# Expert matrices on ScalarE's DMA queue, a joint normalisation of two batches, and one value group per pair of heads, in a Macaron block with experts

## The chip, the cores and the metric

The kernel runs on one core of a Trainium2 chip. A core has five engines that each work through their own instructions in order: TensorE (PE) multiplies matrices and transposes, VectorE (DVE) and ScalarE (ACT) work on rows, GpSimd (POOL) does elementwise work and issues the indirect DMAs, and SyncE (SP) issues the other DMAs. "PEld" in the profile is PE's weight load, which overlaps its products. The engines wait for one another by semaphores. The metric is the device time of one execution in microseconds (us); the median of several runs is given.

## The reference

The input x is 4 batches of 512 rows of 256 numbers, all in float32. LN is a layer norm without weights.

```
x = x + 0.5 * FFN(LN(x));  x = x + ATT(LN(x));  x = x + 0.5 * FFN(LN(x))

FFN(x):  logits = x @ gate                      # 8 experts
         w, e = top_2(logits); w = softmax(w)
         out[row] = sum over its 2 experts of w * ((silu(x @ w0[e]) * (x @ w1[e])) @ wo[e])
                                                # w0, w1: 256x512; wo: 512x256
ATT(x):  q = rms_norm(x @ wq_a) @ wq_b          # 16 heads of 64 + 64 (rope)
         k, v from rms_norm(x @ wkv_a) @ wkv_b  # the rope part of k is shared by all heads
         out = softmax(rope(q) @ rope(k)^T * scale) @ v;   return out @ wo
```

## The kernel before, in words

**FFN.** Each of the two FFNs is worked as 39 tiles of 128 rows, all rows of a tile for one expert. Routing chooses two experts per row, counts the rows of each expert, and lists for each tile its row indices, weights and expert. It runs ahead of the tiles or beside them: for the first FFN batches 0 and 1 come first (`route_first`, L659), nine tiles made of them are begun, and `route_second` (L744) routes batches 2 and 3 beside these tiles. The list of the other 30 tiles can only be read after that.

`ffn_tiles` (L910) is a generator, one tile per step. `gather` (L919) reads the tile's row in the weights into a register, starts the DMAs of w0 and w1 of the expert (512 KB each) and has POOL gather the 128 rows `xg`. It is called two tiles ahead; three buffers hold the weights, so a tile's weights can start when the hidden products of the tile three before are done. `turn` (L946) transposes `xg`; `hidden` (L956) does 32 products into two PSUM tiles `h`, the silu on ACT (L973) and the product on DVE (L975); `project` (L978) does 8 products `py`, scales them on DVE (L998), and POOL adds the rows to `acc_d` in DRAM by an indirect DMA (L1003). `load_x` (L108) reads a batch's x back from `acc_d` on SP, which must wait for those additions. Near the end of the second FFN four DMAs (L1015) copy `acc_d` to the output; the last tiles are then added to the output itself.

**Attention.** An item is one head of one batch, and two items are a pair, with eight steps `at` = 0 to 7 (loop at L1338 to L1384). A step issues in this order: the score group of a row block one and a quarter heads ahead (`put_scores`; two products `ps`, then the negated maximum on DVE, L1163, and the exponential on ACT, L1166), the four transposes of one key chunk of the item's four divided row blocks (`turn_probs`, L1173, copied out of PSUM by DVE or ACT), in some steps the value products (`put_weigh`, L1242) or a half of an output projection (`put_out`), and the division of the row block just scored (`put_divide`: a reciprocal on DVE, L1170, and a multiplication on POOL, L1171). In the value products (`weigh`, L1187) two heads lie side by side in PE's columns, two products a key chunk. The chunks 0 and 1 of a pair are issued as a group at step 7 of the pair, the chunks 2 and 3 at step 1 of the next pair. Every second pair carries an output projection.

**Side work.** `Beside` (L313) holds generators: routing for the second FFN, normalisation of the next batch (`normed`, L411), its keys and values (`prepare`, L1061). Each `step()` lets the first generator issue its next piece. A piece that says `PE_NEXT` wants PE next, and is then let on only at the places given as `pe_places`. In attention there are one or two `step()` calls in each step, ten in a pair: at even steps after the division, at odd ones ahead of it, with a second one after it at steps 1 and 7. `asked` is a second such list, for the queries.

**Normalisation.** `normed` does the row statistics of a batch's four row blocks, an inverse square root by three Newton rounds on DVE (`inv_sqrt`, L362, lines 372 to 374), the normalised rows on DVE (first half) and ACT (second half), their stores to DRAM, the transposes, and the copies out of PSUM. `route_second` calls it for batch 2 and then for batch 3. `list_tiles` (L799) then sums the counts (`pn_c`, L820), and looks rows and weights up by products (`px`, from L876) in a table that it reads back from DRAM.

Of the kernel before, what the change touches and what calls it, by code (L numbers as in the profile page):

```python
# [9 lines left out]
F32 = mybir.dt.float32  # L10
# [6 lines left out]
P = 128  # L17
# [15 lines left out]
def kernel(  # L33
# [48 lines left out]
    tp = ctx.enter_context(tc.tile_pool(name="turned", bufs=1))  # L82
    tm = ctx.enter_context(tc.tile_pool(name="tmp", bufs=2))
    xp = ctx.enter_context(tc.tile_pool(name="xn", bufs=2))
# [3 lines left out]
    ptp = ctx.enter_context(tc.tile_pool(name="pt", bufs=2 * NT))  # L88
# [222 lines left out]
    PE_NEXT = "pe"  # L311

    class Beside:  # L313
        def __init__(self, pe_places=None):
            self.todo = []
            self.pe_places = pe_places
            self.count = self.until = self.place = 0
            self.pe = False

            self.quiet = True  # L320
# [9 lines left out]
        def step(self, n=1):  # L330

            for _ in range(n):
                if not self.todo or self.count < self.until:
                    return
                if self.pe and self.pe_places and self.place not in self.pe_places:
                    return
                said = next(self.todo[0], self)
                self.pe = said is PE_NEXT
                if said is self:
                    self.todo.pop(0)  # L340
                elif said is not None:
                    self.until = self.count + (1 if self.pe else said)
# [14 lines left out]
    def stats(mv, xt, t):  # L357
        sb = small.tile([P, 6], F32, tag="st", name="st")
        nc.vector.bn_stats(sb, xt[:, t, :])
        nc.vector.bn_aggr(mv[:, t, :], sb)  # L360
# [17 lines left out]
    def minus_mean(mv, rstd):  # L378
        less = small.tile([P, NT], F32, tag="less", name="less")
        nc.vector.scalar_tensor_tensor(less, mv[:, :, 0], -1.0, rstd, ALU.mult, ALU.mult)  # L380
        return less
# [29 lines left out]
    def normed(b, s, store=None, then=None, joint=False):  # L411
# [3 lines left out]
        for t in range(NT):  # L415
            stats(mv, xs[b], t)
            yield
# [128 lines left out]
    def choose(ph, s, lTs, b, cut):  # L546
# [47 lines left out]
        yield PE_NEXT  # L594
# [149 lines left out]
    def route_second(ph, listing):  # L744

        s = {}
        lTs = []
        for b in range(2, B):
            yield from normed(b, s, ph.f, joint=True)
            pl = ps_p.tile([P, P], F32, tag="p", name="pl")  # L750
            gate(pl, lambda t: s["xnT"][:, :, t * P : (t + 1) * P])
            lTs.append(ap.tile([P, P], F32, tag="o", name="lT"))
            nc.scalar.copy(lTs[-1], pl)
            yield
        nt = NT * len(lTs)
# [4 lines left out]
        for t in range(0, n, 2):  # L760
            for k in range(2):
# [10 lines left out]
                yield PE_NEXT  # L772
# [26 lines left out]
    def list_tiles(ph, n, m, split=0, read=None):  # L799
# [15 lines left out]
        def parts():  # L815
# [55 lines left out]
            yield PE_NEXT  # L871
# [38 lines left out]
    def ffn_tiles(f, jobs, final=None):  # L910
# [8 lines left out]
        def gather(j):  # L919
            if j >= n:  # L920
# [4 lines left out]
                engines=(mybir.EngineType.SP,),  # L925
# [5 lines left out]
            for w, src in enumerate((w0_k, w1_k)):  # L931
                nc.sync.dma_start(
                    w01[j][:, w],
                    src.rearrange("e k m -> (e k) m")[bass.ds(row, D), :].rearrange(
                        "(c p) m -> p c m", p=P
                    ),
                )
# [361 lines left out]
    beside.step(5)  # L1299
    next(tiles)  # L1300

# [3 lines left out]
    for j in tiles:  # L1305
# [11 lines left out]
        elif j > done + 3:  # L1317
            beside.step()
# [17 lines left out]
    beside.pe_places = None  # L1336
    late = []
    for i, (b, h) in enumerate(items):  # L1338
# [13 lines left out]
        for kc in range(NT):  # L1352
# [9 lines left out]
            if at == 1 and i > 0:  # L1362
                put_weigh(i - 1, (2, 3))
            elif at == 7:
                put_weigh(i, (0, 1))
# [7 lines left out]
            if kc % 2:  # L1373
                beside.step()
            else:
                asked.step()
            put_divide(k)
            if kc % 2:
                asked.step()
                if at in (1, 7):  # L1380
                    beside.step()
            else:
                beside.step()
# [3 lines left out]
    put_weigh(n_items - 1, (2, 3))  # L1387
# [6 lines left out]
    beside.pe_places = PE_PLACES  # L1394
# [76 lines left out]
```

## Time and profile before

| | |
|---|---|
| median of 3 runs | 1213.08 us (1212.36 to 1217.93) |
| the profiled execution | 1213.32 us, of which the span is 1211.3 |
| mean granted clock of PE | 0.969 |
| start to about 46 us | routing of batches 0 and 1, folding of weights |
| 46 to 305 us | first FFN's tiles |
| 317 to 943 us | attention: PE busy 595 of 626 us |
| 947 to 1199 us | second FFN's tiles: PE busy 231 of 252 us |
| hidden products `h`, L963 | 2496 matmuls, 300.9 us |
| scores `ps`, L1155 | 512 matmuls, 271.9 us |
| transposes `pt`, L1177 | 1024, 156.6 us |
| value products `po`, L1190 | 512, 126.1 us |
| weights of the tiles | 156 DMAs of 512 KB on SP's queue |

One line of a timeline is the start in us, the time taken, the engine, the line of the kernel, the operation, what it writes <- what it reads, the shape and the number of instructions put together; in brackets stands how long the engine had been idle before, and what ended that. "SPq" is SP issuing a DMA; the time is that of the issue, not of the transfer. The page's row "PEclk" shows the clock that PE was granted, in tenths of full speed, in 40 equal slices of the span.

### The profile page before, as it was taken

The numbers are of one execution on the slowest core, as the hardware profiler recorded it, in microseconds if no ns is written. First come the engines' busy times: TensorE is split into PE (matmuls) and PEld (weight loads), VectorE is DVE, ScalarE is ACT, GpSimd is POOL, SyncE is SP. The second block draws the span as 40 slices with busy tenths as digits, with TensorE's granted clock in tenths as the row PEclk, the third lists the DMA queues.
The fourth block names the chain that finished last, engine by engine and source line by source line (L and its number), as shares of the span: only waits on it lengthen the run. The fifth ranks groups of instructions, "written<-read, shape, count | busy, mean of one in ns | idle before, by whom it ended". The sixth has DMA issues, their size and how long they took to land. (4 is left out here: it accounts for less than half of the span.)

```text
span 1211.3 us, 18471 instructions
## 1 busy us (share of the span) xinstructions
PE 1107.8 (91%) x6264; PEld 775.0 (64%) x6264; DVE 612.3 (51%) x1677; ACT 406.0 (34%) x914; POOL 577.5 (48%) x645
## 2 busy tenths in 40 slices
PE   4888999799999999999899989999999997999795
PEld 3677999788545455444445545454445787999784
DVE  6463222234567556686657666666755332222121
ACT  4420111011454555453455544455544210101000
POOL 4244444345545554443565435573663254444242
PEclk8989999899999999998999989999999998999898
DMA  9776888665100000100000100000002587887762
GB/s 304 233 220 166 228 246 234 206 201 150 18 1 1 1 1 5 48 1 1 1 1 18 35 1 1 1 18 18 1 5 70 161 231 161 221 238 216 264 207 38
DMA packets 80365, 126.43 MB, mean 104 GB/s; under 512 B 13105, under 2 KB 36785, under 8 KB 80177
## 3 DMA queue, kind: packets, MB, share of 16 engines
q1 hardware_dynamic: 62816, 101.86, 25.7%
q0 software_dynamic: 17184, 23.39, 11.2%
q8 instruction: 51, 0.84, 0.3%
q14 instruction: 42, 0.34, 0.1%
q10 hardware_dynamic: 272, 0.01, 0.0%
HBM read 107.88 MB, written 21.54 MB: 107 GB/s over the span
## 5 line engine op out<-in xcount | busy, mean ns | idle before, releaser
L1171 POOL TENSOR_SCALAR pr<-pr,sm 128x512 f32<-128x512 f32 x256 | 177.8, 696 | 285.5 <-DVE sm L1170 246.4
L963 PE MATMUL h<-xT,w 128*128 128x128 f32 x2496 | 300.9, 280 | 14.1 <-DVE xT L954 5.7
L963 PEld LDWEIGHTS h<-xT,w 128*128 128x128 f32 x2496 | 297.7, 197 | 21.6 <-DVE xT L954 8.0
L1166 ACT ACTIVATE pr<-ps,nm 128x512 f32<-128x512 f32 x256 | 175.9, 687 | 304.5 <-DVE nm L1163 278.5
L1155 PE MATMUL ps<-k,q 128*128 128x512 f32 x512 | 271.9, 614 | 4.5 <-ACT pr L1166 4.5
L1177 PEld LDWEIGHTS pt<-ident,pr 128*128 128x128 f32 x1024 | 126.7, 141 | 157.0 <-issue 98.1
L1163 DVE TENSOR_REDUCE nm<-ps 128x1 f32<-128x512 f32 x256 | 174.7, 683 | 103.5 <-PE ps L1155 103.2
L1003 POOL DMA_INDIRECT acc_d<-yo,idx x64 | 102.0, 1593 | 200.7 <-DVE yo L998 140.8
L973 ACT ACTIVATE g<-h 128x512 f32<-128x512 f32 x78 | 46.5, 596 | 390.6 <-PE h L963 240.4
L975 DVE TENSOR_TENSOR it<-g,h 128x512 f32<-128x512 f32 x78 | 53.6, 687 | 242.8 <-PE h L963 205.0
L1177 PE MATMUL pt<-ident,pr 128*128 128x128 f32 x1024 | 156.6, 276 | 17.0 <-ACT pT L1184 13.8
L989 PE MATMUL py<-wo_sb,it 128*128 x624 | 152.7, 389 | 0.8 <-PE pt_x L951 0.2
L1155 PEld LDWEIGHTS ps<-k,q 128*128 128x128 f32 x512 | 79.7, 191 | 77.4 <-ACT pr L1166 39.4
L989 PEld LDWEIGHTS py<-wo_sb,it 128*128 128x128 f32 x624 | 115.1, 194 | 17.9 <-issue 4.4
L1190 PE MATMUL po<-pT,low 128*64 128x512 f32 x512 | 126.1, 615 | 0.0
L939 POOL DMA_INDIRECT xg<-xn_d,idx x78 | 77.7, 996 | 32.6 <-issue 20.6
L1170 DVE RECIPROCAL sm<-sm 128x1 f32<-128x1 f32 x256 | 41.2, 161 | 101.7 <-ACT pr L1166 101.3
L1182 DVE COPY pT<-pt 128x512 f32<-128x512 f32 x128 | 87.0, 680 | 2.2 <-PE pt L1177 2.2
L1184 ACT COPY pT<-pt 128x512 f32<-128x512 f32 x128 | 73.7, 575 | 2.9 <-PE pt L1177 2.9
L998 DVE TENSOR_SCALAR yo<-py,wt 128x256 f32<-128x256 f32 x78 | 37.7, 483 | 71.0 <-PE py L989 67.1
L1204 PE MATMUL pwo<-wvo,oT 128*128 128x256 f32 x256 | 65.4, 398 | 2.3 <-ACT oT L1252 2.3
L1190 PEld LDWEIGHTS po<-pT,low 128*64 128x64 f32 x512 | 31.6, 138 | 49.0 <-issue 49.0
(218 smaller groups left out, 1003.0 us busy)
## 6 DMA issues: line engine op xcount, KB each, us to landing
w<-in_L_ffn_w_kernel_dram SPq DMA_DIRECT2D x156, 512.0 KB
wo_sb<-in_L_ffn_wo_kernel_dram SPq DMA_DIRECT2D x4, 1024.0 KB
x<-_attn_hidden_states_dram SPq DMA_DIRECT2D x4, 512.0 KB
xn_d<-xn POOLq DMA_DIRECT2D x8, 256.0 KB
x<-acc_d SPq DMA_DIRECT2D x4, 512.0 KB
acc_d<-x SPq DMA_DIRECT2D x4, 512.0 KB
xn_d<-xn SPq DMA_DIRECT2D x8, 256.0 KB
out_dram<-acc_d SPq DMA_DIRECT2D x4, 512.0 KB
```

Of the source, the lines that this page charges most:

```text
L939: nc.gpsimd.indirect_dma_start(out=xg[j], out_offset=None, in_=xn_d[f][: res["rows"], :], in_offset=bass.IndirectOffsetOnAxis(ap=res["idx" ...
L963: nc.tensor.matmul(p[:, m, :], lhsT=w01[j][:, w, c, m * P : (m + 1) * P], rhs=xT[j][:, c, :], start=(c == 0), stop=(c == DC - 1),)
L989: nc.tensor.matmul(py, lhsT=it[:, m, :], rhs=wo_sb[:, bass.ds(off + m * D, D)], start=(m == 0), stop=(m == MC - 1),)
L1003: nc.gpsimd.indirect_dma_start(out=dst, out_offset=bass.IndirectOffsetOnAxis(ap=idx, axis=0), in_=y, in_offset=None, compute_op=ALU.add,)
L1155: nc.tensor.matmul(ps, lhsT=qT[:, t * P : (t + 1) * P], rhs=st[b]["k"][h % 2], start=True, stop=True,)
L1163: nc.vector.tensor_reduce(nm, ps, AX.X, ALU.max, negate=True)
L1166: nc.scalar.activation(pr, ps, AF.Exp, bias=nm, accum_out=sm)
L1171: nc.gpsimd.tensor_scalar(pr, pr, sm, 1.0, ALU.mult, ALU.mult)
L1177: nc.tensor.transpose(pt[:, t * P : (t + 1) * P], probs[t][:, kc * P : (kc + 1) * P], ident)
L1182: nc.vector.tensor_copy(s, pt)
L1184: nc.scalar.copy(s, pt)
L1190: nc.tensor.matmul(po[j * RANK : (j + 1) * RANK], lhsT=st[b]["low"][:, kc, 1, :], rhs=pts[j], start=(kc == 0), stop=(kc == NT - 1),)
```

## The change: what it does

- The register load and the two weight DMAs of a tile are issued by ACT instead of SP.
- `route_second` normalises batches 2 and 3 together: eight statistics, one inverse square root over eight columns, all eight normalised blocks, the four stores on SP; then the transposes of one batch after the other, all copied by ACT, and both gates. Two buffers more hold normalised rows, and one more the transposed ones.
- A second word for side work, `PE_LATE`, lets a piece on at the first of the `pe_places` alone. In `normed` the statistics are issued two at a time. Beside the first tiles eight pieces are let on before the first tile's step and three after it.
- All four key chunks of a pair's value products are one group, issued at step 0 of the next pair; one buffer more holds turned probabilities.
- Side work in attention is let on behind the division only, in the numbers `PARTS` for the eight steps (ten a pair, as before). Beside the last tiles of the first FFN and the tiles of the second, PE work of it is let on at one of a tile's places (1) instead of two (1 and 3).

```
-    tp = ctx.enter_context(tc.tile_pool(name="turned", bufs=1))
+    tp = ctx.enter_context(tc.tile_pool(name="turned", bufs=2))
-    xp = ctx.enter_context(tc.tile_pool(name="xn", bufs=2))
+    xp = ctx.enter_context(tc.tile_pool(name="xn", bufs=4))
-    ptp = ctx.enter_context(tc.tile_pool(name="pt", bufs=2 * NT))
+    ptp = ctx.enter_context(tc.tile_pool(name="pt", bufs=2 * NT + 1))
...
-                if self.pe and self.pe_places and self.place not in self.pe_places:
-                    return
+                if self.pe and self.pe_places:
+                    n_ok = 1 if self.pe is PE_LATE else len(self.pe_places)
+                    if self.place not in self.pe_places[:n_ok]:
+                        return
...
     def route_second(ph, listing):
         s = {}
+        bs = range(2, B)
+        n = NT * len(bs)
+        mv = small.tile([P, n, 2], F32, tag="mv2", name="mv2", bufs=1)
+        for i in range(n):
+            stats(mv, xs[2 + i // NT], i % NT, i)
+            yield
...
+        yield from inv_sqrt(rstd, var, n)
+        less = minus_mean(mv, rstd)
...
+                store_rows(nc.sync, ph.f, b, half, xn[b, half])
...
+        for b in bs:
+            yield PE_LATE if b == 2 else PE_NEXT
+            for half in range(2):
+                pt = ps_p.tile([P, DC, H2 * P], F32, tag="p", name="pt_ln")
+                turn_rows(pt, xn[b, half])
+                xnT[b, half] = pt
+            yield
...
+                nc.scalar.copy(t[:, :, half * H2 * P : (half + 1) * H2 * P], xnT[b, half])
...
+        yield PE_LATE
-        for b in range(2, B):
-            yield from normed(b, s, ph.f, joint=True)
+        for b in bs:
             pl = ps_p.tile([P, P], F32, tag="p", name="pl")
...
-                engines=(mybir.EngineType.SP,),
+                engines=(mybir.EngineType.Activation,),
...
-                nc.sync.dma_start(
+                nc.scalar.dma_start(
                     w01[j][:, w],
...
     beside.at(0)
-    beside.step(5)
+    beside.step(8)
     next(tiles)
+    beside.step(3)
...
         elif j > done + 3:
-            beside.step()
+            beside.pe_places = PE_PLACES[:1]
+            beside.step(2)
...
+    PARTS = (4, 2, 1, 1, 0, 0, 1, 1)
+    beside.pe_places = ()
...
-            if at == 1 and i > 0:
-                put_weigh(i - 1, (2, 3))
-            elif at == 7:
-                put_weigh(i, (0, 1))
+            if at == 0 and i > 0:
+                put_weigh(i - 1, range(NT))
...
-            if kc % 2:
-                beside.step()
-            else:
+            if kc % 2 == 0:
                 asked.step()
             put_divide(k)
             if kc % 2:
                 asked.step()
-                if at in (1, 7):
-                    beside.step()
-            else:
-                beside.step()
+            beside.step(PARTS[at])
...
-    beside.pe_places = PE_PLACES
+    beside.pe_places = PE_PLACES[:1]
```

## The prediction

> **What bounds the kernel now.** I read the page first, then the busy times by stretch, then the timelines of TensorE (PE), of SyncE (SP), and of all engines at the places where PE stood still.
>
> ```profile
> span 1211.3 us, 18471 instructions
> ...
> PE 1107.8 (91%) x6264; PEld 775.0 (64%) x6264; DVE 612.3 (51%) x1677; ACT 406.0 (34%) x914; POOL 577.5 (48%) x645
> ...
> PEclk8989999899999999998999989999999998999898
> ```
>
> PE is the bound, and what a change of order can win is PE's idle time (its gaps sum to 90.9 us) and half clock. The stretches say where:
>
> ```profile
> 50.00:100.00 50.00, 42.14 (x296) 38.56 (x295) 29.42 (x117) 9.64 (x16) 22.87 (x29) 0.90 0.76 214
> ...
> 150.00:200.00 50.00, 50.00 (x382) 48.12 (x381) 13.79 (x28) 5.38 (x9) 23.50 (x19) 1.00 0.89 239
> 200.00:250.00 50.00, 43.61 (x311) 40.64 (x310) 16.29 (x48) 5.74 (x10) 18.06 (x14) 0.93 0.74 211
> ...
> 544.46:573.70 29.24, 26.38 (x98) 14.24 (x96) 17.96 (x43) 12.03 (x29) 10.29 (x13) 0.88 0.00 1
> 615.20:631.26 16.06, 15.97 (x69) 7.42 (x68) 9.74 (x22) 9.15 (x23) 12.71 (x18) 1.00 0.02 2
> ```
>
> Columns: window, length, busy PE, PE weight load, DVE, ACT, POOL, granted clock, DMA share, GB/s. From 150 to 200 us the FFN tiles leave PE no gap and nothing can be won; the first tiles and the tiles at 200-250 do. In attention a pair of heads with no side work has no gap either (615.20), but one beside the next batch's normalisation takes 29.24 at a clock of 0.88.
>
> The stops in the FFN stages, from the timelines of PE and SP (bracket: idle time before and what ended it):
>
> ```profile
> 64.49 3.81 PE L963 MATMUL h<-xT,w 128*128 128x128 f32 x32 [2.47 <-DVE newton L373]
> ...
> 220.39 0.37 SPq L110 DMA_DIRECT2D x<-acc_d  x1
> 221.34 2.47 SPq L932 DMA_DIRECT2D w<-in_L_ffn_w_kernel_dram  x4
> ...
> 233.37 0.69 PE L951 MATMUL pt_x<-ident,xg 128*128 128x128 f32 x2 [6.07 <-DMA xg<-xn_d,idx]
> ...
> 1022.61 0.59 PE L820 MATMUL pn_c<-ones,wide 128*128 128x1 f32 x2 [2.71 <-DVE wide L817]
> ```
>
> The name at 64.49 misleads: the tile's second weights landed at 64.3. At 220 the weights of a tile stand on SP behind an x load that waited for a scatter; at 226.79 the next gather was issued with 2 MB of weights in flight.
>
> The end of a quiet pair, all engines:
>
> ```profile
> 628.07 0.68 DVE L1163 TENSOR_REDUCE nm<-ps 128x1 f32<-128x512 f32 x1
> ...
> 628.43 1.94 PE L1190 MATMUL po<-pT,low 128*64 128x512 f32 x8
> ...
> 628.84 0.69 ACT L1166 ACTIVATE pr<-ps,nm 128x512 f32<-128x512 f32 x1 [0.44 <-DVE nm L1163]
> ...
> 629.65 0.16 DVE L1170 RECIPROCAL sm<-sm 128x1 f32<-128x1 f32 x1 [0.31 <-ACT pr L1166]
> 629.99 0.69 POOL L1171 TENSOR_SCALAR pr<-pr,sm 128x512 f32<-128x512 f32 x1 [0.37 <-DVE sm L1170]
> ...
> 630.30 1.12 PE L1155 MATMUL ps<-k,q 128*128 128x512 f32 x2
> ...
> 631.26 0.60 PE L1177 MATMUL pt<-ident,pr 128*128 128x128 f32 x4
> ```
>
> The first transposes of the next pair need the fourth divided row block, ready at 629.99 + 0.69 = 630.68. PE reaches them at 631.26: slack 0.58. What filled the time was the value group at 628.43.
>
> **The change part by part**, against the profiled execution, 1213.3 (span 1211.3 and 2.0 around it; the median, 1213.08, is 0.2 less).
>
> *A. First tiles.* From 46 to 118 us PE loses 13.3 in gaps and some 7 to half clock. One chain of Newton steps for two batches puts the listing of the remaining tiles about one tile earlier. In the changed program's order the third pair of weight loads is now on ACT ahead of the first silu; it waits for the second wne and nwq loads, which landed at 59.6 and 60.9. So the first silu comes at about 61 instead of 48.49, and the second half of tile 1's hidden products waits for PSUM until about 63: nearly what tile 2 lost before (64.49). Then each further step runs beside a 5.5 us tile, and tile 7's hidden products, at 111.62 (half clock until 113.2), start at about 104. That is -9; taking 2 off because four extra stores and all eight transpose copies are new on SP and ACT: -7, between -11 and 0. ACT's issue itself is about 0.27 + 2 x 0.42 = 1.1 us a tile (its only DMA before took 0.416) on an engine busy for 5.4 of 50 us at 150-200: hidden; uncovered only where it waits.
>
> *B. Tiles at 211-233.* Weights no longer stand behind the x loads: they go out when slots come free, at about 216.2 and 221.7, and the gather finds less in flight: -4 (-6 to 0) of 6.07 + about 2 of half clock. Here the Trainium skill speaks against the change: "DMA: Bandwidth & Descriptors", section "Issuing engines are not separate DMA queues", says that transfers started from any engine share the same 16 DMA engines, and that a second issuer saves only the issue time. The row: SP needs 0.37 per issue, 156 x 0.37 = 58 us, on an engine nobody waits for. By the rule alone this part gives 0. By the rows above the price is the wait in order (the x load's 12.2 us for two), which the rule leaves out. I take the rows, with the rule's 0 as an end.
>
> *C. Second FFN.* The step at 1022.61 has one tile more to come: -2.7 and -1.7 of half clock, less 0.9 for what comes closer behind it, -3.5. Near the end the weights waited on SP behind the four output copies (issued 1118.76; PE idle 5.32 until 1127.52). On ACT they stand behind the first copy's completion, about 1119.5, and hold the silus of one or two tiles: -1 (-4 to +2). Together -4.5 (-8 to +2). The first two weights of this stage now wait for ACT's last attention step, about 936; needed at 948, hidden.
>
> *D. One value group per pair.* It removes an entry and exit: 2 x 1.94 became one of 3.44, with 0.15 and 0.09 less at its borders: -0.33 a pair. But the half at step 7 was the cover shown above. Without it the score group of 630.30 starts at 628.28, PE is ready for the transposes at 629.14, and they start at 630.78: a stop of 1.64. Then 0.53 transposes, 0.15 + 3.44 of products, one score group (0.86), transposes (0.53): the third score group starts at 636.3 instead of 634.96, +1.34. Eight such borders: +10.7. In seven more a side transpose of 0.44 covers part: +0.9 each, +6.3. Sixteen pairs carry an output projection (19.22 us), whose 2.0 us is cover enough: -0.2 each, -3.2. Sum +14 (0 to +20). Low end: the scheduler's side work now fills the place.
>
> *E. Where side work stands.* Its amount per pair is ten steps before and after. Pairs with it cost about 44 us over quiet pairs plus their own matmuls (the two normalising pairs, at 29.24 and 29.17, some 7 each), largely since Newton steps of 0.16 stretched to 1.1 beside POOL's rope additions and stood ahead of a maximum. After the change they fall at steps 0 and 1: -5 in each of the two. Against it, every side step now lies behind a divide and lengthens the chain maximum, exp, reciprocal (1.66 us a step, 628.07 to 629.73) in pairs with little slack, about +1. Sum -9; no row shows side work so placed, so -20 (half of the 44) to +6 (each side step of some 12 pairs in the chain, 0.5 each). I take the value near the normalising pairs, the only rows that show a cause.
>
> *F. Clock.* D adds some 15 stops of about 1.6 us. The skill's "TensorE: Matmul & The Clock Gate", section on the HAM clock gate, asks for a whole idle window of about 3.4 us before the clock halves: by it these cost nothing more. The trace disagrees: of eight stops of 1.7 to 1.9 us in attention three were followed by half clock (497.4: 1.82, then 3.4 us; 548.5 and 712.5: 1.92, then 6.8 us). Half clock over 3.4 us costs 1.7; at a lower chance for shorter stops, 2 of 15: +3 (0 to +8).
>
> Sum: -7 - 4 - 4.5 + 14 - 9 + 3 = -7.5, so 1213.3 - 7.5, about 1206.
>
> **The rivals.** *Slower, about 1222.* One mechanism: the place in front of each pair's first transposes, PE waiting for POOL's divide. It decides once it costs over 1 us in all sixteen pairs without projection and side work pays nothing: +17 from D, +5 for clock, 0 from E, -13 from A to C (15.5, less 2.5 that ACT's waits cost). For it: the slack is 0.58 and the removed cover 1.94. Against it: the side steps. *No change, about 1213.* ACT works in order, so weights that wait for SP's loads or output copies hold silu and with it PSUM; A and C shrink to -4, B to 0 (the skill's rule), and D and E cancel at +4. *Larger gain, about 1193.* The jams of the side-work pairs go (E -16), A to C give 15.5, and D, with F, costs only 11.5. *The change does not do what it says*: the first silu's wait until 61 could take all of A; that is in the no-change case.
>
> **How the numbers follow.** Main case 1206 (1197 to 1214), chance 0.45; slower 0.22; no change 0.18; larger gain 0.15. The range, 1191 to 1224, takes in most of all four. About 0.5% (6 us) is what a measurement of this kernel can tell from no change. Main: 0.28 faster, 0.12 same, 0.05 slower; larger gain: 0.15 faster; no change: 0.02, 0.14, 0.02; slower: 0, 0.03, 0.19. Together 0.45, 0.29, 0.26.
>
> **What would show it.** A: first silu at about 61, PE stopped inside tile 1, tile 7's hidden products at about 104. B: the gap before the tile at 227 down to about 2. C: no gap before pn_c; a gap near the end at a silu, not at weights. D: in quiet pairs without projection a stop of about 1.6 ahead of the first transposes, released by POOL, and a length of about 17.4; with projection unchanged. E: normalising pairs near 24. F: new half clock in attention. I am wrong if the stop in D lies in pairs with projection too, or if side work finds its place in it.

## The result, and the profile after

The changed kernel took 1251.68 us (median of 4 runs, 1243.68 to 1257.07); the kernel before, beside it, 1214.88. The ratio is 1.0296, with a 95% interval of 1.0229 to 1.0363: 3% slower, where 1206 was forecast. Later medians of the kernel before, taken beside the experiments, went from 1214.7 to 1224.9, so every ratio below is against runs of it beside the kernel in question, and stages are compared in the profiles. One profiled execution (weights alone on ScalarE) was a disturbed one: of it only the start and the attention are used.

The page of the changed kernel, the same rows as before:

```profile
span 1246.9 us, 18456 instructions
...
PE 1112.9 (89%) x6264; PEld 781.9 (63%) x6264; DVE 613.1 (49%) x1662; ACT 410.5 (33%) x916; POOL 575.4 (46%) x641
...
PEclk9888999899989999899999989998999999999998
```

The work is the same (6264 matmuls, 5 us more of PE, which half clock stretches); the span is 35.6 longer. By the starts of hidden products and transposes in the two profiles:

| stretch | before | after | difference | forecast |
|---|---|---|---|---|
| start to the first hidden products | 46.4 | 54.3 | +7.9 | 0 |
| first FFN, tiles 0 to 26 | 171.6 | 173.6 | +2.0 | -7 (A) |
| tiles 26 to 28 | 19.5 | 19.6 | +0.1 | -4 (B) |
| tiles 28 to 38 | 67.1 | 77.0 | +9.9 | 0 |
| tile 38 to the first transposes of attention | 12.1 | 12.2 | +0.1 | 0 |
| attention, first to last transposes | 621.4 | 643.8 | +22.4 | +8 (D, E, F) |
| its end, to the second FFN's first products | 10.2 | 9.0 | -1.2 | 0 |
| second FFN, to the end | 263.0 | 257.5 | -5.5 | -4.5 (C) |

How far such a stage can be trusted is seen where kernels share a stage's code. Attention has hardly a DMA in it: it took 620.6 to 622.4 in four kernels with the old attention and 643.7 to 643.9 in three with the new one. The second FFN, with its weights on SyncE, took 260.5 to 270.1 in kernels that do not differ there, and tiles 0 to 26 took 167.5 to 175.7 in seven kernels with the old first FFN; a few us there say nothing. The start is steady (46.0 to 47.1 in these seven), and so is the loss at tiles 28 to 38 (67.1 to 70.0 in these seven, 77.0 to 81.1 in the six kernels that have the new edit there).

Busy times of stretches of the changed kernel (columns as in the prediction): the first is the one after the start, the next two a pair without and a pair with projection, both quiet; the fourth and fifth are pairs with the same work, statistics and Newton steps of the next batch; the last is the pair where the routing's normalisation now stands.

```profile
50.00:100.00 50.00, 40.12 (x281) 36.47 (x280) 22.64 (x94) 13.61 (x22) 15.12 (x20) 0.88 0.76 210
...
477.50:493.51 16.01, 15.80 (x70) 7.38 (x68) 9.45 (x22) 9.54 (x23) 8.55 (x11) 1.00 0.00 0
493.51:513.35 19.84, 19.11 (x84) 10.67 (x85) 11.48 (x27) 10.00 (x26) 10.07 (x13) 1.00 0.00 1
...
513.35:535.88 22.53, 19.74 (x77) 9.57 (x76) 14.83 (x45) 11.01 (x26) 8.56 (x11) 0.85 0.20 70
681.44:701.28 19.84, 16.88 (x77) 8.35 (x76) 14.74 (x45) 11.00 (x26) 8.56 (x11) 1.00 0.26 81
...
724.87:749.22 24.35, 19.60 (x73) 9.47 (x72) 18.76 (x60) 10.64 (x26) 9.37 (x11) 0.86 0.00 0
```

Two quiet pairs take 35.85 where they took 35.28: little. The pairs with side work took the time. The pairs of 29.24 and 29.17 came down to 21.95 and 20.97, but the pairs ahead of them went from 18.18 and 18.17 to 22.63 and 24.35. And of two pairs with the same work the one at a clock of 0.85 takes 2.69 longer than the one at 1.00.

**The start.** Timelines of PE, SP and ACT. The kernel before:

```profile
40.59 2.82 ACT L303 ACTIVATE wvo<-pb,nwk 64x512 f32<-64x512 f32 x4 [5.79 <-PE pb L294]
40.75 2.45 SPq L932 DMA_DIRECT2D w<-in_L_ffn_w_kernel_dram  x4
...
43.77 0.55 SPq L1292 DMA_DIRECT2D acc_d<-_attn_hidden_states_dram  x1
...
45.43 0.44 PE L951 MATMUL pt_x<-ident,xg 128*128 128x128 f32 x2
46.43 3.81 PE L963 MATMUL h<-xT,w 128*128 128x128 f32 x32 [0.56 <-ACT wvo L303]
```

The changed kernel:

```profile
41.35 0.54 SPq L1327 DMA_DIRECT2D acc_d<-_attn_hidden_states_dram  x1
...
41.78 3.01 ACTq L967 DMA_DIRECT2D w<-in_L_ffn_w_kernel_dram  x4
...
45.97 5.69 PE L294 MATMUL pb<-wvo,vT 64*64 64x256 f32 x22 [3.93 <-ACT wvo L303]
51.58 0.44 PE L986 MATMUL pt_x<-ident,xg 128*128 128x128 f32 x2
54.31 5.44 PE L998 MATMUL h<-xT,w 128*128 128x128 f32 x32 [2.29 <-DVE rstd L377]
...
62.68 1.28 ACT L1008 ACT_TABLE_LOAD   x1 [5.60 <-DMA nwq<-n_L_attn_q_a_norm_w_dram]
```

Before, the first weights were issued on SP at 40.75, ahead of the 2 MB copy of x into the accumulator (43.77). By the semaphores of their landings in the trace, the first tile's two landed at 45.0 and 46.4, the second tile's at 48.9 and 50.8. Now the copy goes out at 41.35 on a queue of its own, and the weights, issued from 41.78, land at 54.2, 55.8, 57.6 and 60.0. The four issues also hold ACT for 3 us: its work on wvo, for which PE waits 3.93, begins at 45.23 instead of 40.59, and PE reaches the first tile's transposes (`pt_x`) at 51.58 instead of 45.43. So two delays lie side by side; the weights are the one that ended last. The name at 54.31 (a Newton step) misleads again; and the first silu waits until 62.68 for loads that the third pair of weights, ahead of it on ACT, waits for.

**The tiles at 226 to 240.** POOL in the kernel before (its x load at 220.39 and the stop at 233.37 stand in the prediction):

```profile
224.89 1.59 POOL L1003 DMA_INDIRECT acc_d<-yo,idx  x1 [5.53 <-DVE yo L998]
226.79 0.99 POOL L939 DMA_INDIRECT xg<-xn_d,idx  x1 [0.30 <-issue]
```

ACT, SP, POOL and PE of the changed kernel:

```profile
231.63 0.92 ACTq L967 DMA_DIRECT2D w<-in_L_ffn_w_kernel_dram  x2
231.98 0.36 SPq L110 DMA_DIRECT2D x<-acc_d  x1
...
238.57 1.58 POOL L1038 DMA_INDIRECT acc_d<-yo,idx  x1 [7.54 <-DMA x<-acc_d]
240.46 1.00 POOL L974 DMA_INDIRECT xg<-xn_d,idx  x1 [0.30 <-issue]
...
243.36 0.69 PE L986 MATMUL pt_x<-ident,xg 128*128 128x128 f32 x2 [4.39 <-DMA xg<-xn_d,idx]
```

In both kernels the gather is late because the accumulation ahead of it on POOL waits for the x load to have read the accumulator (the `yo` named at 224.89 belongs to rows that were ready at 218.7). What the weights' queue changes is which of the two is slow. Before, the x loads went out ahead of the weights: the accumulations followed 4.57 and 4.50 us behind the two loads' issues, but PE had the gather of 226.79 only 6.58 us later. Now the loads go out 0.3 to 1.0 us behind weights on the other queue: the accumulations follow after 6.51 and 6.59 us, and the gathers reach PE after 2.87 and 2.90. PE's stops are 1.31 and 4.39, where there was one of 6.07. In the profiles read for this, the accumulation followed after 4.5 to 4.6 us in three kernels with SyncE's queue, and after 6.0 to 7.6 in eight with ScalarE's.

**The first FFN's last tiles.** POOL and PE:

```profile
302.71 1.26 POOL L1092 TENSOR_TENSOR q<-tcos,tsin 64x512 f32<-64x512 f32 x1
304.12 1.02 POOL L974 DMA_INDIRECT xg<-xn_d,idx  x1 [0.15 <-POOL q L1092]
...
308.54 0.69 PE L986 MATMUL pt_x<-ident,xg 128*128 128x128 f32 x2 [3.89 <-DMA xg<-xn_d,idx]
```

With two side steps at a time at one place of a tile, POOL's rope additions of the queries stand in a bunch ahead of the next rows' gather; PE waits 3.89 for it. Over tiles 28 to 38 PE's stops sum to 8.4 us, where they were 2.4, and half clock is 8.8 us longer (an estimate: 4.4 lost).

### The profile page after: what moved, and what is told of

Same layout as the page of the kernel before. It is cut to its first block, busy times and chain, and to the rows that moved or that the text cites. A ratio compares the mean times of both kernels' runs of the same rounds, so it can differ in the third digit from the quotient of the medians.

```text
span 1246.9 us, 18456 instructions
## 1 busy us (share of the span) xinstructions
PE 1112.9 (89%) x6264; PEld 781.9 (63%) x6264; DVE 613.1 (49%) x1662; ACT 410.5 (33%) x916; POOL 575.4 (46%) x641
## 5 line engine op out<-in xcount | busy, mean ns | idle before, releaser
L1198 DVE TENSOR_REDUCE nm<-ps 128x1 f32<-128x512 f32 x256 | 175.1, 684 | 75.4 <-PE ps L1190 74.5
L1038 POOL DMA_INDIRECT acc_d<-yo,idx x64 | 101.7, 1590 | 225.4 <-DVE yo L1033 149.6
L1212 PE MATMUL pt<-ident,pr 128*128 128x128 f32 x1024 | 163.8, 280 | 36.5 <-ACT pT L1219 14.6
L1024 PE MATMUL py<-wo_sb,it 128*128 x624 | 155.3, 394 | 0.5
L1225 PE MATMUL po<-pT,low 128*64 128x512 f32 x512 | 117.6, 601 | 0.0
L1205 DVE RECIPROCAL sm<-sm 128x1 f32<-128x1 f32 x256 | 41.7, 163 | 130.7 <-ACT pr L1201 130.4
L1225 PEld LDWEIGHTS po<-pT,low 128*64 128x64 f32 x512 | 34.3, 137 | 60.0 <-issue 57.0
L1239 PE MATMUL pwo<-wvo,oT 128*128 128x256 f32 x256 | 60.9, 381 | 1.4 <-DVE tsin L1086 1.3
```

The lines of the kernel that those rows point to most:

```text
L1024: nc.tensor.matmul(py, lhsT=it[:, m, :], rhs=wo_sb[:, bass.ds(off + m * D, D)], start=(m == 0), stop=(m == MC - 1),)
L1038: nc.gpsimd.indirect_dma_start(out=dst, out_offset=bass.IndirectOffsetOnAxis(ap=idx, axis=0), in_=y, in_offset=None, compute_op=ALU.add,)
L1198: nc.vector.tensor_reduce(nm, ps, AX.X, ALU.max, negate=True)
L1212: nc.tensor.transpose(pt[:, t * P : (t + 1) * P], probs[t][:, kc * P : (kc + 1) * P], ident)
L1225: nc.tensor.matmul(po[j * RANK : (j + 1) * RANK], lhsT=st[b]["low"][:, kc, 1, :], rhs=pts[j], start=(kc == 0), stop=(kc == NT - 1),)
```

## The experiments

Names: "before +" is the kernel before with one edit, "after +" the changed kernel with one edit. "Attention" is the time from the first to the last transposes in the profile, "half clock" how much of it PE was granted half its clock.

| kernel | ratio to before (95%) | attention, us | half clock, us |
|---|---|---|---|
| before | 1 | 621.4 | 17.0 |
| after | 1.0296 (1.0229 to 1.0363) | 643.8 | 34.0 |
| before + weights on ScalarE | 1.0115 (1.0071 to 1.0158) | 620.6 | 13.6 |
| before + joint normalisation | 1.0041 (1.0006 to 1.0075) | 622.4 | 17.0 |
| before + one value group | 1.0104 (1.0048 to 1.0159) | 626.6 | 10.2 |
| before + side steps as after | 1.0108 (1.0054 to 1.0162) | 629.8 | 20.4 |
| after + first two tiles' weights on SyncE | 1.0164 (1.0126 to 1.0202) | 643.9 | |
| after + last tiles' side work as before | 1.0132 (1.0070 to 1.0194) | 643.7 | |
| after + side steps evenly, behind the division | 1.0308 (1.0268 to 1.0348) | 651.8 | 30.6 |
| after + value group ahead of the transposes | 1.0302 (1.0251 to 1.0353) | 645.2 | 40.8 |
| after + side steps evenly, ahead of the division | 1.0036 (1.0009 to 1.0063) | 615.6 | 3.4 |
| before + all side steps ahead of the division | 0.9883 (0.9818 to 0.9948) | 610.8 | 10.2 |
| before + one value group ahead of the transposes | 1.0042 (1.0018 to 1.0065) | 623.3 | 20.4 |
| before + second FFN's weights on ScalarE | 0.9975 (0.9942 to 1.0007) | 620.6 | |
| after + its own side steps, ahead of the division | 1.0024 (0.9990 to 1.0058) | 613.0 | 3.4 |
| before + side steps ahead, second FFN's weights on ScalarE | 0.9893 (0.9849 to 0.9936) | 610.7 | |
| the same + one group ahead of the transposes | 0.9900 (0.9852 to 0.9947) | 613.3 | 20.4 |
| after, four losses mended | 0.9801 (0.9766 to 0.9837) | 607.0 | 0 |
| the same, again | 0.9793 (0.9761 to 0.9826) | 605.9 | 0 |
| the same, with two value groups | 0.9725 (0.9686 to 0.9764) | 597.2 | 0 |

### One part alone

**Weights on ScalarE**, all of them:

```
-                engines=(mybir.EngineType.SP,),
+                engines=(mybir.EngineType.Activation,),
...
-                nc.sync.dma_start(
+                nc.scalar.dma_start(
```

> The kernel before, with nothing changed but the issuer of the tiles' weights (ScalarE instead of SyncE). My theory: 3 to 7 us slower. The first hidden products start about 8 us later (54 instead of 46), because the weights of the first tiles no longer stand ahead of the 2 MB copy of x into the accumulator on SyncE's queue but compete with it, and because ScalarE's issues push its own wvo products back; the first silu is held until about 63 by loads that the third pair of weights waits for; against it the second FFN's last tiles gain 5 us. Rival (my prediction's parts B and C): the start is hidden and the kernel gains 5 to 10 us.

1.15% slower, about 14 us. The first hidden products start at 52.7 (46.4 before). The part forecast as a gain (B, C, and a piece of A) is a loss by itself. How much of it lies behind the start this run's profile cannot tell.

**Joint normalisation** (`route_second`, its buffers, `PE_LATE`, 8 and 3 pieces; weights on SyncE):

> The kernel before, with the joint normalisation of batches 2 and 3 alone (and its places and buffers); weights stay on SyncE. Theory: the step was right in itself and was hidden by the weights on ScalarE: 5 to 9 us faster, the tile after the first nine's list earlier, first hidden products still at 46. Rival: the table's read-back falls beside the same tile as before and nothing is won, 0 to 2 us.

No gain: 0.4% slower, tiles 0 to 9 in 78.0 us (before 77.8). The third pair of weights, behind the attention's loads and now also the four stores on SyncE, held tile 2 for 7.51 us, and the list came at the same tile as before. My theory of a gain of its own fell; the rival's 0 to 2 us was nearer.

**One value group** at step 0 of the next pair:

```
-            if at == 1 and i > 0:
-                put_weigh(i - 1, (2, 3))
-            elif at == 7:
-                put_weigh(i, (0, 1))
+            if at == 0 and i > 0:
+                put_weigh(i - 1, range(NT))
```

> The kernel before, with all four key chunks of a pair's value products in one group at step 0 of the next pair, side work as before. Theory (from the two traces' quiet pairs, 35.28 and 35.84 us for two): 9 us slower in attention, half clock windows aside; the stop lies ahead of the last of the first four transposes in pairs with an output projection. Rival: the group takes the whole loss in attention, 20 us or more. Second rival (my prediction): 14 us, with the stop in pairs without projection.

Attention 5.2 us longer, with 6.8 us less of half clock; with half of each kernel's half clock taken off (612.9 and 621.5), 8.6 longer, as the theory of 9 had it. The stop is this one in the changed kernel:

```profile
494.75 0.33 PE L1212 MATMUL pt<-ident,pr 128*128 128x128 f32 x1 [0.73 <-POOL pr L1206]
495.01 3.65 PE L1225 MATMUL po<-pT,low 128*64 128x512 f32 x16
```

Three of the four first transposes ran ahead, and the last alone waited for POOL's division. It stands at the end of a pair without projection, where the prediction put it, but counts in the next pair, since that one's first transposes have begun.

**Side steps as after** (numbers 4, 2, 1, 1, 0, 0, 1, 1, all behind the division; statistics two at a time):

```
-            if kc % 2:
-                beside.step()
-            else:
+            if kc % 2 == 0:
                 asked.step()
             put_divide(k)
             if kc % 2:
                 asked.step()
-                if at in (1, 7):
-                    beside.step()
-            else:
-                beside.step()
+            beside.step(PARTS[at])
```

> The kernel before, with the side work of attention let on behind the division in the numbers 4, 2, 1, 1, 0, 0, 1, 1 (and the statistics two at a time); value groups as before. Theory: 10 to 13 us slower, since normalised rows are now waited for by their own transposes (2.6 us in the pairs that begin a normalisation) and side steps lengthen the chain of maximum, exponential and reciprocal. Rival (my prediction's part E): 9 us faster, the two pairs of 29 us shrinking to 24 or less with nothing in return.

Attention 8.4 us longer. The two pairs of 29 us came down to 21.4, 7.8 each and more than forecast, but the pairs before them went from 18.2 to 22.3, and the four pairs that begin a normalisation lost 3.7 to 4.5 each. In each of these PE stops for 3.4 to 3.6 us ahead of `pt_ln`, and half clock follows.

### The changed kernel, one part undone

**The first two tiles' weights back on SyncE** (the queue is chosen by `f == 0 and j < 2`):

> The changed kernel, with the weights of the first FFN's tiles 0 and 1 back on SyncE's queue, ahead of the 2 MB copy of x into the accumulator; all later tiles' weights stay on ScalarE. Theory: 7 to 8 us faster than the changed kernel: the first hidden products at 46 to 47 again instead of 54, and the distance from there to tile 7 unchanged or shorter. Rival (it is the transfers being slow beside the other loads, not the queue order): the first hidden products stay at 52 or later.

The first hidden products start at 47.5 instead of 54.3, and tile 9 comes 75.3 us behind them (78.9 after, 77.8 before). So the start was lost by moving these weights. The run gives back both their place ahead of the copy and ACT's free time (`pt_x` at 46.09 instead of 51.58), and so does not divide the 7 us between the two. What the joint normalisation and ScalarE's queue gain from there is hardly above the spread: tiles 0 to 9 took 72.9 to 76.2 in the four kernels with this start, and 73.7 to 81.6 in seven with the old first FFN; 7 was forecast.

**The last tiles' side work as before:**

```
         elif j > done + 3:
-            beside.pe_places = PE_PLACES[:1]
-            beside.step(2)
+            beside.step()
```

> The changed kernel, with the side work beside the first FFN's last tiles let on as before (one piece a step, PE work at two places of a tile). Theory: tiles 29 to 38 take 61 us again instead of 70, since GpSimd's rope additions of two query pieces no longer stand ahead of the gather of the next rows: 8 us faster than the changed kernel. Rival (weights on ScalarE, behind the queries' copies, cause it): no difference.

Tiles 28 to 38 take 65.6 us instead of 77.0, with the weights still on ScalarE. So this edit was the cause, and the weights' queue was not; that it works by the rope additions is read from the trace above. (The ratios of this run and the last are 20 and 16 us under the changed kernel's, more than the 11 and 7 of their stages; the intervals just allow for that.)

**The side steps evenly**, still behind the division:

```
-    PARTS = (4, 2, 1, 1, 0, 0, 1, 1)
+    PARTS = (1, 2, 1, 1, 1, 1, 1, 2)
```

> The changed kernel, with side work in attention still behind the division but evenly, 1, 2, 1, 1, 1, 1, 1, 2 instead of 4, 2, 1, 1, 0, 0, 1, 1. Theory: the loss from side work is the bunch of four pieces at step 0 (statistics and the whole Newton chain, 5 us of VectorE in a row, ahead of the next maximum): attention 7 us shorter, and up to 8 more by less half clock. Rival (every side step behind a division lengthens the chain): no gain, or slower.

A miss: attention is 8 us longer, not 7 shorter (the ratios, 1.0308 and 1.0296, do not tell the two apart). The bunch of four was not the cause. But this run made a sharp comparison possible: in numbers it is the kernel before, whose attention with one value group took 626.6, and it differs from that one chiefly in that all steps stand behind the division (the statistics are also issued two at a time). It takes 651.8.

**The value group ahead of the first transposes:**

```
+            if at == 0 and i > 0:
+                put_weigh(i - 1, range(NT))
             pts[i, kc] = turn_probs(probs[i], kc)
...
-            if at == 0 and i > 0:
-                put_weigh(i - 1, range(NT))
-            elif at == 2 and h % 4 == 0 and i > 1:
+            if at == 2 and h % 4 == 0 and i > 1:
```

> The changed kernel, with the one value group of a pair put ahead of the first transposes of step 0 instead of behind them, so that it covers the wait for the last divided row block. Theory (lost cover): two quiet pairs take 35.1 us instead of 35.8, the 0.7 us stop gone, 8 us in all. Rival (the 3.5 us between two score groups starves the chain of maximum and exponential wherever the group stands): no gain, the stop turns up later in the pair.

Half a miss. Two quiet pairs take 34.87 us, better than expected and than before; but each pair that begins a normalisation now has a stop of 4.9 instead of 2.6, and half clock is 40.8 us. In all nothing is won.

### The place of the side steps

**Evenly and ahead of the division**, to be set against the run "evenly, behind":

```
-            if kc % 2 == 0:
-                asked.step()
-            put_divide(k)
-            if kc % 2:
-                asked.step()
-            beside.step(PARTS[at])
+            for _ in range(AHEAD[at]):
+                beside.step()
+            if kc % 2 == 0:
+                asked.step()
+            put_divide(k)
+            if kc % 2:
+                asked.step()
```

> The changed kernel with the side work of attention let on ahead of the division in every step (1, 2, 1, 1, 1, 1, 1, 2 pieces), which differs from the even run behind the division in the order alone. New theory: the free place of VectorE is between a maximum and its reciprocal, where it waits 0.9 us for the exponential; a piece behind the reciprocal stands ahead of the next maximum and lengthens the chain of scores. Then attention takes 625 to 632 us instead of 652 (the even run) or 644 (the changed kernel). Rival (the place does not matter, the loss is the group's and the clock's): 644 to 652.

615.6 instead of 651.8: 36 us from the place of one call. **The changed kernel's own numbers, ahead:**

> The changed kernel with its own numbers of side pieces (4, 2, 1, 1, 0, 0, 1, 1), all let on ahead of the division instead of behind it; nothing else. If the place decides whatever the numbers: attention about 616 us, as with the even numbers ahead. If the bunch of four at step 0 costs by itself (5 us of VectorE in a row): 625 to 635. If neither: 644 as in the changed kernel.

613.0 instead of 643.8. The place decides, whatever the numbers. This is the cleanest pair of runs in the study, so here is the same pair of heads in both. Behind the division (the changed kernel):

```profile
683.82 0.16 DVE L1205 RECIPROCAL sm<-sm 128x1 f32<-128x1 f32 x1 [0.31 <-ACT pr L1201]
683.90 0.41 DVE L362 BATCH_NORM_STATS2 st<-x 128x6 f32<-128x256 f32 x1
...
685.55 1.12 PE L1190 MATMUL ps<-k,q 128*128 128x512 f32 x2
...
688.79 0.16 DVE L383 SCALAR_TENSOR_TENSOR less<-mv,rstd 128x4 f32<-128x4 f32 x1
688.87 0.68 DVE L1198 TENSOR_REDUCE nm<-ps 128x1 f32<-128x512 f32 x1
...
690.46 0.16 DVE L1205 RECIPROCAL sm<-sm 128x1 f32<-128x1 f32 x1 [0.91 <-ACT pr L1201]
690.54 1.10 DVE L396 TENSOR_SCALAR xn<-x,mv,rstd 128x256 f32<-128x256 f32 x2
...
690.99 0.33 PE L410 MATMUL pt_ln<-ident,xn 128*128 128x128 f32 x1 [2.58 <-DVE xn L396]
```

Ahead of it:

```profile
669.58 0.69 DVE L1198 TENSOR_REDUCE nm<-ps 128x1 f32<-128x512 f32 x1
...
670.79 0.42 DVE L362 BATCH_NORM_STATS2 st<-x 128x6 f32<-128x256 f32 x1
...
675.55 0.15 DVE L1205 RECIPROCAL sm<-sm 128x1 f32<-128x1 f32 x1
675.62 0.67 DVE L1198 TENSOR_REDUCE nm<-ps 128x1 f32<-128x512 f32 x1
676.21 0.85 DVE L396 TENSOR_SCALAR xn<-x,mv,rstd 128x256 f32<-128x256 f32 x2
...
676.80 0.86 PE L410 MATMUL pt_ln<-ident,xn 128*128 128x128 f32 x4 [1.03 <-DVE xn L396]
```

DVE works in order. Behind the reciprocal, the bunch begins only once the exponential is done (683.82), and the next maximum, whose scores were issued at 685.55, has to wait until 688.87. Ahead of it, the bunch begins while ACT still has the exponential to do; measured from the pair's first transposes (681.44 and 668.79) it begins at 2.00 instead of 2.46, and the next maximum comes at 6.83 instead of 7.43. The normalised rows (`xn`) no longer wait for another exponential (0.91) behind that maximum: they come at 7.42 instead of 9.10. PE's stop falls from 2.58 to 1.03, and the pair from 19.84 to 17.91. With the shorter stops half clock goes too, from 34.0 us to 3.4: an estimate, taking half its length, is 15 of the 31 us.

The pages show the same over the whole run: DVE's idle time ahead of the reciprocals is 101.7 before, 130.7 in the changed kernel, and 106.1 with its steps ahead:

```profile
L1170 DVE RECIPROCAL sm<-sm 128x1 f32<-128x1 f32 x256 | 41.2, 161 | 101.7 <-ACT pr L1166 101.3
...
L1205 DVE RECIPROCAL sm<-sm 128x1 f32<-128x1 f32 x256 | 41.7, 163 | 130.7 <-ACT pr L1201 130.4
...
L1205 DVE RECIPROCAL sm<-sm 128x1 f32<-128x1 f32 x256 | 41.1, 161 | 106.1 <-ACT pr L1201 105.5
```

The two even runs go from 132.8 to 100.2. Ahead of the maxima, where it waits for PE's scores, DVE also stands idle (75.4 in the changed kernel, 72.3 with the steps ahead). That work put there costs so much more is read from this one pair of heads, and not shown for the others.

**All side steps ahead, in the kernel before:**

> The kernel before with all side pieces of attention ahead of the division; before, those of even steps stand behind it. If the place decides as in the run above: attention 5 to 15 us shorter than 621. Rival (five pieces behind the division cost nothing because PE has other cover there): within 3 us of 621.

Attention 610.8, 10.6 less than before, and 1.2% of the whole time: the place is worth something there too.

**One value group with its cover, in the kernel before:**

> The kernel before with one value group a pair, put ahead of the first transposes of step 0, so that it covers the wait for the last division. From the changed kernel with the same move: two quiet pairs 34.9 us instead of 35.3 (before) or 35.8 (group behind the transposes), so attention, half clock windows aside, 3 to 6 us shorter than before. Rival: pairs with side work lose what the quiet ones gain, as they did in the changed kernel.

The rival held: 34.9 us for two quiet pairs, but attention 623.3, 1.9 longer. Pairs with side work lose more than the quiet ones gain.

**The second FFN's weights on ScalarE:**

> The kernel before with the weights of the second FFN alone on ScalarE. In the profiles the second FFN took 254 to 261 us with this queue and the other edits, and 263 to 270 with SyncE's. If the queue is the cause: 4 to 8 us faster in this stage. Rival (the later listing steps and places do it, or the transfers' own spread): no gain.

This stage took 260.1 us, hardly under the 260.5 to 270.1 of SyncE's, and 254.5 to 266.6 in the other undisturbed kernels with ScalarE's; the ratio's interval holds 1. Not shown to gain.

### Together

> The kernel before with all side pieces of attention ahead of the division and the second FFN's weights on ScalarE. If both gains are real and add: 1196 to 1203, about 15 us under the kernel before. If the queue gains nothing: as the run with the side pieces alone, 1.2% under it.

0.9893: no better than the side steps alone (0.9883). The queue gains nothing that these runs can tell.

> As the run before this one, and one value group per pair ahead of the first transposes. If the group with its cover gains in quiet pairs (0.4 us in two) and the side pieces, now off the chain, no longer lose it: 1193 to 1200. Rival (the group makes the scores come in bursts, and pairs with side work pay): 3 to 8 us slower than without it.

0.9900: no gain; attention is 2.6 longer with the group than without, near the rival's 3, which the ratios cannot tell from nothing.

**The changed kernel with the four losses mended** (first two tiles' weights, last tiles' side work, group ahead of the transposes, side steps evenly and ahead of the division; the edits as above):

> The changed kernel with each found loss mended: weights of the first two tiles on SyncE, side work beside the first FFN's last tiles as before, the group ahead of the transposes, side pieces evenly and ahead of the division. If the four losses account for the result, the rest of the change (joint normalisation, ScalarE's queue) shows what it is worth: 1190 to 1205. If something else in it costs: above 1213.

0.9801, and 1198.68 us is in the expected range: no further loss of the whole change shows. That left the group.

> The mended changed kernel, but with the value products in two groups (steps 7 and 1) as before. If the one group ahead of the transposes is worth what quiet pairs show (34.9 against 35.3 us for two): 3 to 6 us slower than the mended kernel. Rival (the side work's pairs gain from the two groups): equal or faster.

> The mended changed kernel once more, beside the run with two groups on the same chip: again 1.6 to 2.3% under the kernel before.

With two groups, at steps 7 and 1 as before, 0.9725 against 0.9793 on the same chip, attention 597.2 against 605.9. The rival held: the one group loses 1.6 us in each pair that begins a normalisation (19.20 against 17.64) and in others with side work, and wins 0.4 in two quiet pairs. The kernel with two groups is the fastest of all, 2.75% under the kernel before (1180.35 us), and its page reads:

```profile
span 1177.3 us, 18440 instructions
...
PE 1090.7 (93%) x6264; PEld 766.2 (65%) x6264; DVE 600.5 (51%) x1662; ACT 407.1 (35%) x916; POOL 574.7 (49%) x641
```

PE is busy for 17 us less than before with the same matmuls, 10.6 of it in attention, which has no half clock.

Against "before + all side steps ahead", with the same groups and the same place of the steps, attention is 13.6 us shorter (597.2 against 610.8). Of that, 9.6 lie in the two pairs that took 29 us before: 22.72 each against 27.50. The runs point to an edit without a line in the forecast, the statistics of `normed` two at a time. The other that differs, more buffers, is also in the run with the joint normalisation alone, which has the statistics one by one and keeps these pairs at 29.3 and 29.2.

## Why the prediction was wrong, step by step

**A, first tiles (-7; measured +9.9 up to tile 26).** The prediction saw that ACT would issue the first weights, and that the first silu would come at about 61 (it came at 64; tile 7's hidden products at 121.4, not 104). It said of the issue "hidden; uncovered only where it waits", and it did not look at what the weights had been ahead of, nor at what their issue would stand ahead of. On SyncE they stood before a 2 MB copy; on a queue of their own they run beside it, and on ACT they hold up the work on wvo. Together that is +7.9, undone by the run with two tiles on SyncE (47.5), which does not divide the two. Of the -7 along the chain little is seen, since the list came beside the same tile's hidden products; the other +2.0 is within the spread.

**B, tiles at 211 to 233 (-4; measured 0).** Half of the step came true: the gather found less in flight, 2.9 us instead of 6.58. What failed is "the price is the wait in order (the x load's 12.2 us for two)". The order had also kept weights from running beside the x loads; without it POOL's accumulation, which waits for each load, came 2.0 us later twice, and the gather stands behind it on POOL. The prediction has no term for that. The rule that I weighed against the rows ("DMA: Bandwidth & Descriptors", section "Issuing engines are not separate DMA queues": transfers from any issuer share the same 16 engines, and a second issuer saves the issue time only) gave 0, and 0 it was; the kernel with only the second FFN's weights moved, at 0.9975 (0.9942 to 1.0007), fits it too.

**C, second FFN (-4.5; measured -5.5).** The size agrees, but kernels that do not differ in this stage spread over 9 us there, and the queue alone showed no gain. Not confirmed; the agreement may be luck.

**D, value group (+14; measured +5.2 alone, +8.6 without the clock).** The mechanism was right, the size not. In the sum all four first transposes wait for the last divided block, a stop of 1.64; three of them ran ahead and one waited, 0.73. So two terms were mis-sized. Between the third score groups of a pair without projection and of the next one the time went from 16.07 to 16.99, +0.92 where I had +1.34; in the other half from 19.21 to 18.86, -0.35 where I had -0.2. Together +0.57 in two quiet pairs instead of +1.14. That putting the group ahead of the transposes removes it (34.87) is shown too.

**E, side work (-9; measured +8.4 alone).** This is the step that decided. It said that "every side step now lies behind a divide and lengthens the chain", put that at "about +1", and set -5 against it in each of two pairs. In the run with the side steps alone, the two pairs gained 7.8 each; ten others paid 1.6 to 4.5 each, 33 together, where I had +1; the rest gained 9. So the price was underrated by far. In the changed kernel the same place costs 31, about 15 of it as half clock. The row that shows a free place stood in the profile before, DVE's idle time ahead of the reciprocals, "<-ACT pr" (0.3 us ahead of about half of them, 0.9 ahead of a quarter), and I read it as part of the chain, not as a place for work. The gain was put down to the wrong edit as well: I had it from the steps' new places ("After the change they fall at steps 0 and 1"), but with the steps spread evenly and ahead they take 27.5 with the statistics one by one and 22.7 with them two at a time. The range of this step ended at +6.

**F, clock (+3; measured about +8.5).** Half clock in attention went from 17.0 to 34.0 us, half of it lost by estimate. I had counted the stops of D, but those were 0.7. Neither part alone brings it: half clock is 10.2 with the group and 20.4 with the side steps. With half of it taken off, the two parts (+8.6 and +6.7) nearly add up to the changed kernel's attention (+13.9); the clock is what they bring together. The rule of the skill ("TensorE: Matmul & The Clock Gate", section "Part 1: The HAM clock gate", which has the clock fall after an idle window of about 3.4 us) would have given 0. Of the four stops of 2.56 to 2.72 ahead of `pt_ln`, which end at 362.4, 522.9, 691.0 and 857.4, three stand at half-clock windows of 6.8 us that begin at 362.1, 522.5 and 857.0; the other 13.6 us come 1 us behind stops of 2.14 and 1.48, and within a row of stops that begins with one of 2.14. The measurement decides here: shorter stops do it, though not each time.

**What had no step at all.** The edit beside the first FFN's last tiles cost 10 us (11.4 by the run that undoes it). The prediction lists no cost for it. It issues two query pieces at a time, whose additions are POOL's, ahead of POOL's gathers; every instruction that a moved step issues has to be counted, also those of an engine that is not named in the edit.

The rival "slower, about 1222" had the right sign and the wrong mechanism: it laid the loss on the transposes' wait in all pairs without projection, which is worth 9 us at most. What stays open: what the second FFN owes to ScalarE's queue, how the start's loss divides between the copy and ACT, and whether the joint normalisation gains anything. Whether an x load can be put where no accumulation waits for it was not tried.

## What to carry to other kernels

When work is fitted beside a chain that runs round several engines in order, look for the places in each engine's round where it waits for another, and try the work there: the same ten pieces cost 31 us more on the other side of one reciprocal. When a transfer is moved to another queue, ask what it had stood ahead of on the old one, not only what it had waited behind, and what its issue will hold up on the new one. And list every edit of a change with what it issues on every engine, the small ones beside the main stages too; here one without a line in the forecast cost 10 us.

## What the runs showed of the hardware that was not expected

Half clock set in at the end of stops of about 2.6 us in three of four cases, came in stretches of 3.4 or 6.8 us, and cost 2.69 us in a pair of heads with 6.8 us of it (22.53 against 19.84 with the same work). With the same steps ahead of the division these stops were 1.0 to 1.2 us, and none was followed by it; nor were four of 1.7 to 1.8 us elsewhere in that attention, of whose 613 us 3.4 were at half clock. And beside a transfer of 2 MB (and the loads behind it) issued 0.4 us ahead on another queue, four weight transfers of 512 KB landed 12.4 to 15.9 us after their issue; on one queue, issued ahead of that transfer, they had taken 4.2 to 7.9.
